# Tying a background task, scores, counts and running sums' products to their place in the list

## The chip, the core and the metric

The kernel runs on one core of a Trainium2 chip. A core has five engines with a queue of instructions each: TensorE (PE, products), VectorE (DVE, elementwise work), ScalarE (ACT, functions and copies), GpSimd (POOL, here mostly the issue of transfers) and SyncE (SP, transfers only). An engine takes its instructions strictly in the order in which the program lists them for it. The metric is the device time of one execution in microseconds (us), as a median over several executions.

## What is computed

A matrix of features `x` of 2708 x 512 goes through four layers on one weighted graph `adj` of 2708 x 2708, all in fp32. Every layer ends in a residual sum and a layernorm. Cut to what matters here:

```python
deg = maximum((adj != 0).sum(-1), 1.0)               # how many neighbours each row has
# layer 0: x = layernorm(x + (inc @ x) / inc.sum(-1)), with inc made from adj
# layer 1:
type_sum = adj @ x                                   # the gates' input and the second branch
h = x @ W_sa
s_left, s_right = h @ a_sa[0, :512], h @ a_sa[0, 512:]        # the scores
e = where(adj != 0, exp(-leaky_relu(s_left[:, None] + s_right[None, :], 0.01)), 0.0)
attn = e / (e.sum(axis=1, keepdims=True) + 1e-05)    # e.sum: the running sums
x_a, x_b = attn @ h, adj @ (x @ W_gcnb) + b_gcnb
x = layernorm(x + sigmoid(gate_a * x_a + gate_b * x_b))
# layer 2: x = layernorm(x + sum over hops k of adj^k @ x @ weight[k])
# layer 3: a_norm = rsqrt(deg) * (adj + I) * rsqrt(deg);  x = layernorm(x + relu((a_norm @ x + x) @ W + b))
```

## The kernel before

`adj` is taken as 2 x 2 blocks of half its size (1354). A product with it is made as seven products of half size over sums and differences of the blocks (s1 to s4), where eight would be direct. The result columns are cut into ranges: in the layer-1 sweeps 384, 384, 256 and 330 columns. One range takes seven *slots*, one for each product, in the order P1, P7, P5, P6, P4, P3, P2; a slot is 10 steps of k (128 rows of `adj`), each with two instructions per half (`step`, L462, "a row" is four of these), and what is over 1280 rows follows in `rest` (L480, L486). TensorE accumulates in banks `accu`, `accc`, `accd`, `acca`; ScalarE copies them out (L516), VectorE adds them into the tiles C11 to C22 and their sums (`add`, L523; names such as `P1c`, `C21`, `W`), and dense products (`dense`, `ps_d`, L610) multiply these by the weights.

The kernel is written as a list. `at(pos, fn, hold=False)` (L179) puts a function down at a position, counted in slots; at the end the list is sorted by position and the functions are called in that order (L1723). A scheduler then orders the instructions of each engine by its own estimates of when they are ready and how much depends on them, so the order in the program is not the order of the list. The exception is `hold`: every instruction that such a function issues gets an order-only dependence on the instruction that stands before it on the same engine in the list (L1730). It can't be put ahead of that one, while instructions of functions without `hold` may still move.

The stages are at positions `S = [0, 28, 35, 91, 119, 147, 175]` (L687): layer 0, the plain product of layer 1 for the last range (S[1]), the attention of layer 1 (S[2], four ranges of seven slots), and then the later layers. The change touches S[1] and S[2]:

- `score` (L902): VectorE multiplies a tile of x by the score vectors and sums along the row (L907); `score_rows` (L929) turns a column of scores into a row (`to_rows`, L921: TensorE transpose `ps_r` L924, ScalarE copy, POOL store); SyncE loads those rows again for the attention.
- `pair` in `extra1` (L970): signs (ScalarE L973), squares (L974) and counts (VectorE L980) of the last range, for `deg`.
- In S[2] each block of `adj` is masked: ScalarE makes `e` (L1143, L1144), VectorE multiplies (L1145), makes s1 to s4 (`comb`, L407) and adds up running sums over rows (`add_run`, L766 to L770). `run_sums` (L777) reduces those over partitions by products with a vector of ones (`rs`, L783), for h=1 and h=0 of each range.
- The *background task* (L1048 to L1129) runs in S[2] beside the attention: for the 512 columns of each of two groups, ten rounds of k and one of the rest. A round: `back_load` (four transfers of 256 KB issued on POOL, L1059, into the tiles bk_0 to bk_3, which have one buffer each), `back_tally` (signs L1072, squares L1073 on ScalarE, counts `dg` L1075 on VectorE), `back_sums` (four VectorE operations L1095 which overwrite the tiles, and four stores to DRAM on POOL, L1096, which later layers load as `z<-As`). The next round's loads need those tiles and so the stores' end. A group ends with `back_end` (TensorE products `ds`, L1103) and `back_rows`.

Of the kernel before, what the change touches and what calls it, by code (L numbers as in the profile page):

```python
# [25 lines left out]
P = 128  # L26
EPS = 1e-5
NH = 1354
KT = 11
# [32 lines left out]
def wt(k):  # L62
    return min(P, NH - k * P) if k < KT else P
# [8 lines left out]
def gnn_kernel(ctx: ExitStack, tc: tile.TileContext, x, adjT, w_sa, a_sa, w_gcn, b_gcn, wab, bab, w_hop, w_out,  # L72
# [106 lines left out]
    def at(pos, fn, hold=False):  # L179

        def go():
            n = len(nc.cur_bb.bb.instructions)
            fn()
            held.update(range(n, len(nc.cur_bb.bb.instructions)))

        events.append((pos, len(events), go if hold else fn))
# [590 lines left out]
    def run_sums(R0, n, h, after):  # L777

        ps = bank("rs", [P, 4])
        t = run.pop((R0, h))  # L780
        ts = list(range(R0 // P, (R0 + n + P - 1) // P))
        for i, k in enumerate(ts):
            nc.tensor.matmul(ps[: wt(k), i : i + 1], t[:, k * P - R0 : k * P - R0 + wt(k)], ones_f, start=True,  # L783
                             stop=True)
        r = small.tile([P, 4], F32, name="rd", bufs=4)
        for i, k in enumerate(ts):
            after(r[: wt(k), i : i + 1], ps[: wt(k), i : i + 1], h * KT + k, wt(k))
            rd[h * KT + k] = r[:, i : i + 1]
# [113 lines left out]
    def score(t, w, got, js):  # L902
        x1 = got.pop(t)
        junk = nat("vy")
        for j in js:
            for e in range(2):
                nc.vector.scalar_tensor_tensor(junk[:w, :HD], x1[:w, e * HD : (e + 1) * HD], 1.0, V[j, e][:w],  # L907
                                               ALU.mult, ALU.mult, accum_out=sc2[:w, t, e, j : j + 1])
# [20 lines left out]
    def score_rows(R0, h, ts):  # L929
        q = slice(h * KT + ts[0], h * KT + ts[-1] + 1)  # L930
        to_rows(s_left[:, q], len(ts), SROW[R0, h])
# [8 lines left out]
    got1 = {}  # L940
# [5 lines left out]
    for R0, n in RANGES:  # L946
        full = R0 == RANGES_A[0][0]
        for h in (1, 0):
            ts = tiles_of(R0, n)
            for k in ts:  # L950
                p = S[1] + 0.55 + 0.21 * i
                at(p, lambda t=h * KT + k: get_x1(t))
                at(p + 0.25, lambda t=h * KT + k, w=wt(k), js=range(4 if full else 2): score(t, w, got1, js))
                i += 1
            at(p + 0.26, lambda a=(h * KT + ts[0], len(ts), False): scores_end(*a))
            if full:
                at(p + 0.26, lambda a=(h * KT + ts[0], len(ts), True): scores_end(*a))
            at(p + 0.8, lambda R0=R0, h=h, ts=ts: score_rows(R0, h, ts))
    at(p + 0.27, scores_over)
    for i, (h, k) in enumerate((h, k) for g in (4, 0) for h in (0, 1) for k in range(g, g + 4)):  # L960
        p = S[2] + 1.6 + 1.3 * i
        at(p, lambda t=h * KT + k: get_x1(t))
        at(p + 0.4, lambda t=h * KT + k: score(t, P, got1, (2, 3)))
        if k % 4 == 3:
            at(p + 0.41, lambda a=(h * KT + k - 3, 4, True): scores_end(*a))

    def extra1(pb, r, R0, n, A):
        ts = tiles_of(R0, n)

        def pair(keys, w=P):  # L970
            m = pool.tile([P, 2, D], BF, name="sg", tag="nat", bufs=6)
            for h, key in enumerate(keys):
                nc.scalar.activation(m[:w, h, :n], A[(r,) + key][:w, :n], AF.Sign)  # L973
            nc.scalar.activation(m[:w, :, :n], m[:w, :, :n], AF.Square)  # L974
            if R0 not in deg:
                deg[R0] = d = pool.tile([P, 2, D], BF, name="dg", tag="nat", bufs=6)
                nc.vector.tensor_copy(d[:w, :, :n], m[:w, :, :n])
            else:
                d = deg[R0]
                nc.vector.tensor_tensor(d[:w, :, :n], d[:w, :, :n], m[:w, :, :n], ALU.add)  # L980

        for k in range(KW):
            at(pb + 0.1 + 0.8 * k / KT, lambda k=k: pair((("11", k), ("21", k))))
            at(pb + 3.9 + 0.8 * k / KT, lambda k=k: pair((("12", k), ("22", k))))
        for key, w in (("r", KA), ("r32", 32)):
            at(pb + 4.8, lambda key=key, w=w: pair(((key, 0), (key, 1)), w))

        def end(h):
            d = deg[R0]
            ps = bank("ds", [P, 4])  # L990
            for i, q in enumerate(ts):
                wq = wt(q)
                nc.tensor.matmul(ps[:wq, i : i + 1], d[:, h, q * P - R0 : q * P - R0 + wq], ones_bf[:, 0:1], start=True,
                                 stop=True)
            for i, q in enumerate(ts):
                wq = wt(q)
                o = rdeg[:wq, h * KT + q : h * KT + q + 1]
                nc.vector.tensor_scalar(o, ps[:wq, i : i + 1], 1.0, None, ALU.max)
                nc.vector.tensor_scalar(diag[:wq, h, q : q + 1], o, 1.0, None, ALU.add)
                nc.vector.reciprocal(o, o)  # L1000

        def rows(h):
            to_rows(rdeg[:, h * KT + ts[0] : h * KT + ts[-1] + 1], len(ts),
                    DROW[h][0, ts[0] * P : (ts[-1] + 1) * P].rearrange("(k i) -> k i", i=P))

        at(pb + 5.2, lambda: end(1))
        at(pb + 5.9, lambda: rows(1))
        at(pb + 5.2, lambda: end(0))
        at(pb + 5.9, lambda: rows(0))
# [81 lines left out]
    def back_sums(i0, k):  # L1091
        a11, a21, a22, a12 = back["t"]
        for m, o, a, b, op in (("s1", a22, a21, a22, ALU.add), ("s3", a21, a11, a21, ALU.subtract),
                               ("s2", a11, a22, a11, ALU.subtract), ("s4", a12, a12, a11, ALU.subtract)):
            nc.vector.tensor_tensor(o, a, b, op)  # L1095
            nc.gpsimd.dma_start(out=SD[m][k * P : (k + 1) * P, i0 : i0 + D], in_=o)  # L1096

    def back_end(i0):
        d = back.pop("d")
        ps = bank("ds", [P, 8])  # L1100
        for h in range(2):
            for i in range(4):
                nc.tensor.matmul(ps[:, 4 * h + i : 4 * h + i + 1], d[:, h, i * P : (i + 1) * P], ones_bf[:, 0:1], start=True,  # L1103
                                 stop=True)
        for h in range(2):
            q = slice(h * KT + i0 // P, h * KT + i0 // P + 4)
            o = rdeg[:, q]
            nc.vector.tensor_scalar(o, ps[:, 4 * h : 4 * h + 4], 1.0, None, ALU.max)
            nc.vector.tensor_scalar(diag[:, h, i0 // P : i0 // P + 4], o, 1.0, None, ALU.add)
            nc.vector.reciprocal(o, o)  # L1110

    def back_rows(i0, h):
        q = h * KT + i0 // P
        to_rows(rdeg[:, q : q + 4], 4, DROW[h][0, i0 : i0 + D].rearrange("(k i) -> k i", i=P))

    p = S[2] + 1.3
    for i0, _ in RANGES_B:
        at(p, back_start)
        for k in range(KW):
            at(p, lambda i0=i0, k=k: back_load(i0, k))  # L1120
            at(p + 0.6, back_tally)
            at(p + 0.7, lambda i0=i0, k=k: back_sums(i0, k))
            p += 1.13
        at(p, lambda i0=i0: back_rest_load(i0))
        at(p + 0.6, back_rest_tally)
        at(p + 0.85, lambda i0=i0: back_end(i0))
        at(p + 0.9, lambda i0=i0: back_rows(i0, 0))
        at(p + 0.95, lambda i0=i0: back_rows(i0, 1))
        p += 1.13  # L1129

    def start2b():
# [15 lines left out]
    def extra2(pb, r, R0, n, A):  # L1147
        def rows(h):
            row[R0, h] = tmp("row")
            m = (n + P - 1) // P  # L1150
            src = SROW[R0, h][0:1, :]
            nc.sync.dma_start(out=row[R0, h][:, : m * P].rearrange("p (k i) -> p k i", i=P),
                              in_=bass.AP(tensor=src.tensor, offset=src.offset, ap=[[0, P], [P, m], [1, P]]))

        def share(o, s, t, w):
            nc.vector.tensor_scalar(o, s, 1e-5, None, ALU.add)
            nc.vector.reciprocal(o, o)
            if R0 == RANGES_A[0][0]:
                nc.vector.tensor_tensor(o, o, gate[:w, t, 0:1], ALU.mult)

        at(pb - 1.6, lambda: rows(0))
        at(pb - 1.0, lambda: rows(1))
        at(pb + 5.2, lambda: run_sums(R0, n, 0, share))
        at(pb + 4.7, lambda: run_sums(R0, n, 1, share))

    def finish_x2(y, x1, w, t, h, r0):

# [562 lines left out]
    for n, i in enumerate(list(nc.cur_bb.bb.instructions)):  # L1730
        p = last if n < 3 * strict else done if n in held else {}
# [44 lines left out]
```

## Time and profile before

| | |
|---|---|
| median of 3 runs | 2932.55 us (2932.35 to 2941.14) |
| the profiled execution | 2930.68 us, span 2928.9 us, mean granted clock 0.988 |
| busy: TensorE, VectorE, ScalarE, POOL | 97%, 78%, 23%, 22% of the span |
| layer-1 sweeps S[1] and S[2] in the trace | about 434 to 552 us, and 552 to 1017 us |
| TensorE busy in 400 to 1000 us, by windows of 100 us | 91.4, 97.6, 95.7, 94.0, 90.5, 85.2 us |

A line of the profile names an engine, the operation, its output `<-` its inputs, and the line of the kernel. A wait reads: engine, tile and line that waited, `<-` the engine, tile and line that released it. "x8" means so many instructions. `bk`, `sg` and `dg` are the background task's tiles (`sg` and `dg` also name those of `pair`), `run` is a running sum, `a` a block of `adj`, and `As` is where the background task stores.

### The profile page before, as it was taken

The page shows a single profiled execution, that of the slowest core. Times are in us where ns is not written, and L with a number is a line of the kernel's source. Part 1 is how long each engine was busy: PE and PEld are TensorE (multiplying, and loading weights), DVE is VectorE, ACT ScalarE, POOL GpSimd, SP SyncE. Part 2 cuts the span into 40 slices and gives each one's busy share as a digit, 9 for nine tenths or more (in the row PEclk, how much of TensorE's full clock was granted, in tenths as well). Part 3 has the DMA queues.
Part 4 walks back from the last instruction along what each step waited for, and adds up shares of the span by engine and source line. Part 5 has one row for each costly group of instructions (what it writes and reads, how often), then busy time and mean ns, then how long its engine had stood idle before and what let it go on. Part 6 is the DMA issues. An engine that isn't in the chain of part 4 may idle for free.

```text
span 2928.9 us, 38864 instructions
## 1 busy us (share of the span) xinstructions
PE 2832.2 (97%) x11159; PEld 1913.9 (65%) x11159; DVE 2292.8 (78%) x5890; ACT 661.3 (23%) x1314; POOL 650.8 (22%) x1175
## 2 busy tenths in 40 slices
PE   7999999999989899999999999999999999999998
PEld 5655666556576678777666666666666666656665
DVE  6898688676667657677599877987878877899986
ACT  4554214765557311201200000000000100100001
POOL 0123233222232210213202224021230221501102
PEclk9999999999999999999999999999999999999999
DMA  7666466466566565577767768566675565854652
GB/s 225 194 204 186 140 206 205 138 206 190 168 203 197 164 183 146 176 221 244 228 177 240 211 196 257 166 184 213 192 251 165 177 202 176 251 152 138 182 140 79
DMA packets 404959, 554.41 MB, mean 189 GB/s; under 512 B 68752, under 2 KB 350556, under 8 KB 404744
## 3 DMA queue, kind: packets, MB, share of 16 engines
q1 hardware_dynamic: 330976, 391.33, 45.8%
q0 software_dynamic: 56032, 148.83, 15.4%
q10 hardware_dynamic: 17736, 11.76, 1.4%
q8 instruction: 89, 1.46, 0.2%
q14 instruction: 126, 1.03, 0.1%
HBM read 468.02 MB, written 83.65 MB: 188 GB/s over the span
## 4 chain that ended last, share of the span: by engine, by line
PE 71%; DVE 12%; issue 6%; DMA 6%; POOL 3%; ACT 1%; SPq 1%; POOLq 0%; DVEq 0%; ACTq 0%
PE accd L1356 13%; PE accu L1356 13%; PE accc L1356 12%; PE ps_d L610 6%; PE acca L1356 6%; PE accd L462 4%; PE accc L462 3%; PE accr L1427 3%; PE accu L462 3%; DMA bk<-in_adjT 2%; PE acca L462 2%; DVE z L1301 2%; DMA As<-bk 1%; PE accr L1431 1%; PE ps L649 1%
## 5 line engine op out<-in xcount | busy, mean ns | idle before, releaser
L1301 DVE TENSOR_TENSOR z<-z 128x339 f32<-128x339 f32 (+2 forms) x1176 | 538.4, 490 | 20.4 <-PE accu L1356 10.6
L1374 ACT COPY q<-accu 128x339 f32<-128x339 f32 (+2 forms) x105 | 41.6, 429 | 1056.7 <-PE accu L1356 836.2
L1356 PE MATMUL accc<-s,t 128*128 128x339 f32 (+2 forms) x784 | 233.5, 439 | 0.2 <-DVE s L1301 0.2
L1356 PE MATMUL accu<-z,t 128*128 128x339 f32 (+2 forms) x784 | 227.7, 436 | 4.2 <-DVE z L1301 3.0
L1356 PE MATMUL accd<-z,t 128*128 128x339 f32 (+2 forms) x784 | 227.8, 436 | 1.7 <-DVE q L1438 1.4
L1356 PE MATMUL accc<-z,t 128*128 128x339 f32 (+2 forms) x784 | 226.8, 436 | 0.5 <-ACT q L1374 0.5
L564 POOL TENSOR_TENSOR rstd<-rstd,neg_half 128x1 f32<-128x1 f32 (+3 forms) x91 | 59.7, 656 | 702.0 <-DVE rstd L563 446.9
L1356 PEld LDWEIGHTS accu<-z,t 128*128 128x128 f32 x784 | 148.1, 190 | 70.1 <-DVE z L1301 6.1
L1356 PEld LDWEIGHTS accc<-s,t 128*128 128x128 f32 x784 | 146.8, 190 | 70.7 <-issue 10.2
L1356 PEld LDWEIGHTS accd<-z,t 128*128 128x128 f32 x784 | 148.1, 190 | 66.7 <-DVE q L1438 2.3
L1356 PEld LDWEIGHTS accc<-z,t 128*128 128x128 f32 x784 | 148.2, 190 | 64.8 <-ACT q L1374 1.0
L1380 DVE TENSOR_TENSOR q<-q,accd 128x338 f32<-128x338 f32 (+2 forms) x140 | 67.9, 485 | 148.3 <-PE accd L1356 148.0
L1301 DVE TENSOR_TENSOR s<-z 128x339 f32<-128x339 f32 (+2 forms) x392 | 178.0, 490 | 7.5 <-PE accc L1356 3.2
L1575 POOL DMA_DIRECT2D Y<-y x192 | 104.7, 552 | 330.0 <-DVE y L1570 289.2
L407 DVE TENSOR_TENSOR a<-a,a 128x384 f32<-128x384 f32 (+2 forms) x240 | 118.0, 516 | 5.3 <-DMA a<-in_adjT 4.3
L1143 ACT ACTIVATE e<-row,s_right 128x384 f32<-128x384 f32 (+5 forms) x176 | 94.8, 566 | 41.0 <-DVE a L1145 11.6
L1145 DVE SCALAR_TENSOR_TENSOR a<-a,e 128x384 f32<-128x384 f32 (+2 forms) x160 | 76.9, 508 | 34.1 <-ACT e L1144 34.0
L569 ACT ACTIVATE ld<-ld,rstd 128x512 f32<-128x512 f32 (+3 forms) x45 | 36.5, 813 | 263.9 <-DVE rstd L566 98.1
L1438 DVE TENSOR_TENSOR q<-q,accr 128x338 f32<-128x338 f32 (+2 forms) x160 | 69.1, 485 | 22.8 <-PE accr L1431 22.7
L1380 DVE TENSOR_TENSOR q<-q,accu 128x338 f32<-128x338 f32 (+2 forms) x175 | 79.2, 485 | 3.9 <-ACT q L1374 2.6
L774 DVE SCALAR_TENSOR_TENSOR s<-a,row 128x384 f32<-128x384 f32 (+2 forms) x152 | 75.3, 508 | 6.0 <-ACT row L759 6.0
L1144 ACT ACTIVATE e<-e 128x384 f32<-128x384 f32 (+5 forms) x176 | 78.9, 475 | 1.4
(699 smaller groups left out, 5907.5 us busy)
## 6 DMA issues: line engine op xcount, KB each, us to landing
z<-As SPq DMA_DIRECT2D x320, 169.5 KB
z<-As SPq DMA_DIRECT2D x320, 169.0 KB
z<-in_adjT SPq DMA_DIRECT2D x240, 169.5 KB
z<-in_adjT SPq DMA_DIRECT2D x240, 169.0 KB
a<-in_adjT SPq DMA_DIRECT2D x160, 192.0 KB
bk<-in_adjT POOLq DMA_DIRECT2D x80, 256.0 KB, 4.6
As<-bk POOLq DMA_DIRECT2D x80, 256.0 KB, 3.2
z<-As SPq DMA_DIRECT2D x160, 128.0 KB
```

The source lines that it names most:

```text
L407: nc.vector.tensor_tensor(A[r, dst, k][:, :n], A[r, a, k][:, :n], A[r, b, k][:, :n], op)
L462: nc.tensor.matmul(B[home, c][:, :n], X[STAT[p], k][:, c * P : (c + 1) * P], A[r, MOV[p], k][:, :n], start=bool(start and k == k0), stop=k ...
L610: nc.tensor.matmul(o, lhs(c), r, start=c == 0 and n == 0, stop=c == DC - 1, skip_group_check=True)
L774: nc.vector.scalar_tensor_tensor(t[:w, :n], a[:w, :n], 0.0, row[R0, h][:w, :n], ALU.is_gt, ALU.mult)
L1143: nc.scalar.activation(e[:w, :n], row[R0, h][:w, :n], AF.Prelu, bias=s_right[:w, t : t + 1], alpha=0.01)
L1144: nc.scalar.activation(e[:w, :n], e[:w, :n], AF.Exp, scale=-1.0)
L1145: nc.vector.scalar_tensor_tensor(a[:w, :n], a[:w, :n], 0.0, e[:w, :n], ALU.not_equal, ALU.mult)
L1301: nc.vector.tensor_tensor(d[:, :n], Z[x + (k,)][:, :n], Z[y + (k,)][:, :n], op)
L1356: nc.tensor.matmul(B[home][:, :n], stat(v, k), a[:, :n], start=bool(start and k == 0), stop=k == nk - 1, skip_group_check=True)
L1380: nc.vector.tensor_tensor(d[:, :n], s_[:, :n], B[home][:, :n], ALU.add)
L1427: nc.tensor.matmul(ps[r][:, :n], XA[:KA, c * P : (c + 1) * P], R[h, s][:KA, :n], start=True, stop=False, skip_group_check=True)
L1575: nc.gpsimd.dma_start(out=rows[:, :, f * P : (f + 1) * P], in_=o[32 * f : 32 * (f + 1), : m * P].rearrange("p (b d) -> p b d", d=P))
```

## The change

Functions of the list get `hold=True`, and some positions move. What they issue is the same as before.

```diff
-            at(p + 0.8, lambda R0=R0, h=h, ts=ts: score_rows(R0, h, ts))
+            at(p + 0.8, lambda R0=R0, h=h, ts=ts: score_rows(R0, h, ts), True)
...
-        at(p + 0.4, lambda t=h * KT + k: score(t, P, got1, (2, 3)))
+        at(p + 0.4, lambda t=h * KT + k: score(t, P, got1, (2, 3)), True)
...
-            at(pb + 0.1 + 0.8 * k / KT, lambda k=k: pair((("11", k), ("21", k))))
-            at(pb + 3.9 + 0.8 * k / KT, lambda k=k: pair((("12", k), ("22", k))))
+            at(pb + 0.1 + 0.8 * k / KT, lambda k=k: pair((("11", k), ("21", k))), True)
+            at(pb + 3.9 + 0.8 * k / KT, lambda k=k: pair((("12", k), ("22", k))), True)
         for key, w in (("r", KA), ("r32", 32)):
-            at(pb + 4.8, lambda key=key, w=w: pair(((key, 0), (key, 1)), w))
+            at(pb + 4.8, lambda key=key, w=w: pair(((key, 0), (key, 1)), w), True)
...
             at(p, lambda i0=i0, k=k: back_load(i0, k))
-            at(p + 0.6, back_tally)
-            at(p + 0.7, lambda i0=i0, k=k: back_sums(i0, k))
+            at(p + 0.65, back_tally, True)
+            at(p + 0.75, lambda i0=i0, k=k: back_sums(i0, k), True)
             p += 1.13
         at(p, lambda i0=i0: back_rest_load(i0))
-        at(p + 0.6, back_rest_tally)
-        at(p + 0.85, lambda i0=i0: back_end(i0))
-        at(p + 0.9, lambda i0=i0: back_rows(i0, 0))
-        at(p + 0.95, lambda i0=i0: back_rows(i0, 1))
+        at(p + 0.65, back_rest_tally, True)
+        at(p + 0.9, lambda i0=i0: back_end(i0), True)
+        at(p + 1.1, lambda i0=i0: back_rows(i0, 0), True)
+        at(p + 1.12, lambda i0=i0: back_rows(i0, 1), True)
...
-        at(pb + 5.2, lambda: run_sums(R0, n, 0, share))
-        at(pb + 4.7, lambda: run_sums(R0, n, 1, share))
+        at(pb + 6.5, lambda: run_sums(R0, n, 0, share), True)
+        at(pb + 5.05, lambda: run_sums(R0, n, 1, share), True)
```

`pb` is the first slot of a range and `p` runs on by 1.13 slots from round to round, from S[2] + 1.3 on. `rest` of h=1 is at pb + 5.0 and of h=0 at pb + 5.999, both unchanged. In the new program's order on TensorE, the `rs` of h=1 stands behind `rest` and one row of P3, where it stood ahead of the second half of P4; the `rs` of h=0 stands inside P2.

## The prediction

> **What bounds the kernel now.** I read the page first (TensorE is busy for 97% of the span), then the windows, then TensorE's waits and its timeline in the stage that the change edits, then the chain that leads to the longest of those waits. The windows (start:end and length in us, busy us of each engine with instructions, granted clock, DMA share, GB/s):
>
> ```profile
> core 0: us, PE busy (x) PEld busy (x) DVE busy (x) ACT busy (x) POOL busy (x), PEclk, DMA share, GB/s
> 800.00:900.00 100.00, 90.51 (x412) 74.89 (x411) 66.76 (x195) 62.18 (x130) 30.94 (x58) 0.95 0.65 203
> 900.00:1000.00 100.00, 85.16 (x329) 60.44 (x328) 69.98 (x178) 51.14 (x98) 28.02 (x53) 0.91 0.63 189
> 1000.00:1100.00 100.00, 100.00 (x421) 73.99 (x420) 55.62 (x145) 17.95 (x34) 16.18 (x26) 1.00 0.55 159
> ```
>
> From 1000 us on TensorE is full at clock 1.00, so a microsecond won or lost before that reaches the end one to one. The other windows from 400 us on read 91.4, 97.6, 95.7 and 94.0 busy: 45.6 us of TensorE idle in 400 to 1000, which is all that there is to win. TensorE's waits in 380 to 1020 us (what waits, for what: us in total, times, longest):
>
> ```profile
> PE rs L783 <- DVE run L770: 21.1, 4, 8.7
> PE ds L1103 <- DVE dg L1075: 6.7, 1, 6.7
> PE ps_d L610 <- ACT sg L1073: 6.0, 1, 6.0
> PE ps_r L924 <- DVE s_left L918: 4.8, 2, 4.5
> PE ps_n L593 <- DVE P1c L523: 3.7, 1, 3.7
> ```
>
> The first row is the running sums' product, four times, once in each range of the attention layer. Its timeline (start, us, line, in brackets the idle time before it):
>
> ```profile
> 630.50 1.04 PE L783 MATMUL rs<-ones_f,run 128*128 128x1 f32 x6 [4.28 <-DVE run L770]
> 631.40 4.29 PE L462 MATMUL accc<-a,T4D 128*128 128x384 f32 x8
> 758.05 1.41 PE L783 MATMUL rs<-ones_f,run 128*128 128x1 f32 x6 [5.97 <-DVE run L770]
> 870.66 0.98 PE L783 MATMUL rs<-ones_f,run 128*128 128x1 f32 x4 [8.72 <-DVE run L770]
> 914.18 1.19 PE L610 MATMUL ps_d<-T1B,P1c 128*128 128x256 f32 x2 [5.97 <-ACT sg L1073]
> 984.90 0.37 PE L1103 MATMUL ds<-ones_bf,dg 128*128 128x1 bf16 x8 [6.73 <-DVE dg L1075]
> ```
>
> The second line is what a wait costs afterwards: the same eight products took 2.74 us just before it. What made the sum late is in the chain of waits:
>
> ```profile
> 614.44 3.84 DMA As<-bk
> ...
> 618.57 5.90 DMA bk<-in_adjT
> ...
> 624.49 0.63 ACT sg L1072
> ...
> 628.58 1.87 DVE run L770 x4
> ...
> 630.50 1.04 PE rs L783 x6
> ```
>
> VectorE stood on a background tally (one store, then one load into the same buffer, then signs, square, add), and the last four running-sum adds were behind it. So the background round is a closed loop with one set of buffers, and TensorE meets it through VectorE's order.
>
> **What the Trainium skill says.** "Trainium Architecture — The Big Picture", section "Inside one NeuronCore": each engine has its own instruction stream and they meet only in semaphores. Hence what stands behind a waiting instruction waits too; the chain agrees (run behind dg). "TensorE: Matmul & The Clock Gate", Part 1: the clock is halved after an idle window of about 3.4 us, and wants about as long to come back. The trace agrees: 4.29 against 2.74 us behind a wait of 4.28. "DMA: Bandwidth & Descriptors", section on the SWDGE path: 2.0 us plus bytes over 436 GB/s, which makes an estimated 2.6 us for a 256 KB tile; the page of this kernel has medians of 3.2 (store) and 4.6 (load) and the chain 3.84 and 5.90, so I take the trace's.
>
> **The round, by rows.** From the issue of a round's last store (613.24) to the next tally's add (626.48) the chain has 13.2 us: store 3.84, load 5.90, sign 0.63, square 1.07 (L1073, at 625.38), the rest issue. With one add (L1075, 0.69 mean) and four sums (L1095, 0.69 each) behind it that is 13.2 + 3.4 = 16.7 us for a round in strict order. The timeline of VectorE has the last sums of rounds 11 to 20 and the last add from 821.7 to 984.8: 16.3 us each. TensorE goes through a round's 1.13 slots in 14.6 us at 384 columns (40 rows of four products at 1.29 us are 4 slots, 12.9 us each), 13.6 at 256 and 16.3 at 330. So in the last ranges the loop is the slower of the two.
>
> **The change, part by part.** No instruction is added or taken away: the counts of the two programs are equal on every engine, and the orders are equal up to about 415 us of the trace and, but for numbering, from about 1015 us on.
>
> *Layer-1 sweep (434 to 552 us): scores, score rows, pairs.* VectorE is at 80% in 400 to 500. The C-copies and adds come earlier there, so most of the 3.66 us wait of L593 at 440.24 goes, but the score rows (L924, waits 4.8 + 2.1) stand one to three rows (1 to 4 us) later behind the same VectorE work. I take -1.5 (from -5, both waits gone, to +1). The rows' stores on POOL and their loads on SP move with them; the attention layer reads them tens of us later, so they cost nothing; without that cover a row's store and load would stand in the path with some 8 us.
>
> *Range 0 (384 columns).* The product of h=1 now stands behind T4D, the rest and one row of B22A: about 7 us of TensorE later (T4D 2.74; the rest at L480 and L486 2.9 and 1.1, by the timeline at 635.53 to 639.1; a part of a row). Its sum, at 630.5 before, is met at 633: the wait of 4.28 and the cold clock (4.29 - 2.74 = 1.55) go, 5.8 us. What is late next: the add for C21 (L523) now stands on VectorE behind round 2's sums, and the dense product ps_d (L610) waits for it. Queued behind that add on VectorE are the add for W and the mask products of the next slot (L1145), which TensorE has in stock for a row or two. TensorE would be there at 641.7 - 5.8 = 635.9, the add is there at about 638, and a wait of over 2 us costs about 1 of clock: -2.7.
>
> *Range 1.* The wait of 5.97 and about 2 of clock go, so ps_d would come at 770.6 - 8 = 762.6. But C21 is now behind round 9's first tally. Round 6 ended at 723.8; three rounds at 16.7, less what overlaps, put that tally at about 770.5 to 772.4 (round 9 ended at 770.1 before). So a wait of about 9 us stands there, and the range loses 2.2 with its cold clock.
>
> *Ranges 2 and 3 (256 and 330 columns).* The waits of 8.72 and 0.78 turn into waits for C21 and W, behind round 14's sums (5.5 to 6.5); the wait at 914.18 stays (P1c stands behind round 16's sums, 6 to 7). They don't add up, since the account is settled at ds, where TensorE waited 6.73 before. Rounds of 16.7 in place of 16.3 and the 1.8 of round 9 put the last tally's add at 984.8 + 1.8 + 11 x 0.45 = about 992, 7 us later. Ahead of ds TensorE now has about 8 us more to do (T4D, rest, two rows), which it no longer has to do behind it. Together -0.8 against before, with a bound of -10 to +10, since a round that is 1 us shorter or longer counts ten times.
>
> *Background stores and row stores* on POOL are tied too: the four stores of a round now go out together before the next loads, which moves no landing by more than an issue of 0.54 us. SP's queue is not tied.
>
> *Sum.* Up to ps_d of range 1: -1.5 - 2.7 + 2.2 = -2.0. At ds: -0.8. Work that no longer follows a cold ds (rs, h=1) and what the first ranges give the loop earlier: 1 to 2. I take -3. The profiled execution (2930.68, span 2928.9) would go to 2927.7; the median shown is 1.9 above it, so **2929.5 us**. A difference under 0.3% (8.8 us) is about what a measurement of this kernel can't tell from none.
>
> **Rivals.** *A, the waits are gone for good.* VectorE's main work now stands ahead of each tally, so TensorE never meets the loop. For it: the rs waits are caused by order alone. Against: ds must follow the last tally, and the loop's own 16.3 us is no order's doing. It gives -21.1, and -6.0 of clock (four waits at 1.5), ds and the rest left as they are: about 2905. It needs rounds of under 15.5 us. *B, slower: each round gets longer.* The fixed order makes a round's store, load, both tallies and sums strictly follow each other, behind main operations that themselves wait for TensorE; at 16.7 + 1.5 = 18.2 a round, ten rounds end 19 us later than before, less 3 to 8 us of work moved ahead of ds: +12 to +16, about 2946. It decides from some 17.3 us a round. For it: VectorE in order behind adds that wait for TensorE, and TensorE behind them. Against: the main operations ahead are ready early in most rounds. *C, nothing changes:* unlikely, since the orders differ by whole rows in this stage.
>
> **How the numbers follow.** My case 0.44, A 0.27, B 0.28, C 0.01. My case has a spread of about 7 us around -3, which puts two tenths beyond -8.8 and little beyond +8.8: faster 0.27 + 0.09, slower 0.24 + 0.02, the rest of 0.38 within 0.3%. The range takes B to 2954 and half of A, from 2905 on. The likeliest case alone: 2920 to 2939.
>
> **What would show it.** Right: the waits of rs for run L770 fall from 21.1 to under 4; waits of ps_d L610 for C21 or W (DVE L523) of 15 to 25 us appear; ds waits 8 to 14; the sum of TensorE's idle in 400 to 1000 us stays within 40 to 48; last sums of rounds 11 to 20 are 16.5 to 17.3 apart. Wrong by A: rounds under 15.5 and windows 800 to 1000 over 95% busy. Wrong by B: rounds over 17.5, ds after 998, and DVE bk L1095 waiting for work that stands ahead of it and waits for TensorE. The prediction would also fail if the layer-1 sweep lost time, which I price at little.

## The result, and the profile after

The changed kernel takes 2939.78 us (median of 20 runs, 2932.93 to 2945.09), the kernel before beside it 2932.21 (20 runs, 2924.17 to 2941.14). The ratio is 1.0027, 95% interval 1.0019 to 1.0035: slower by 0.27%, some 7.6 us. That is inside the 0.3% that I had set as too small to tell, but with 20 runs each it can be told, and its sign is not the one of my 2929.5. The profiled execution took 2940.72 us with a span of 2938.9.

The windows of the changed kernel, with the columns as shown before:

```profile
400.00:500.00 100.00, 85.80 (x334) 57.48 (x333) 75.82 (x274) 21.67 (x51) 41.52 (x76) 0.93 0.72 220
...
900.00:1000.00 100.00, 81.50 (x315) 57.61 (x314) 76.10 (x182) 64.41 (x127) 30.99 (x58) 0.92 0.72 219
1000.00:1100.00 100.00, 100.00 (x431) 74.84 (x432) 52.50 (x153) 18.79 (x35) 19.57 (x33) 0.98 0.54 154
```

TensorE's idle time in 400 to 1000 us is 59.9 us, 45.6 before. Stage S[2] alone, from its first to its last product (which ends at 1029.5 us in the trace before, not at about 1017 as stated above), takes 486.1 us, 477.1 before; of the 9.0 us more, 8.5 are idle time of TensorE (43.1 against 34.6). From 1000 us on TensorE is full in both; the clock of 0.98 in that window comes right after the last wait, which ends at 1000.0. The waits of TensorE in 380 to 1040 us:

```profile
PE ps_d L610 <- DVE C L523: 24.3, 3, 11.4
PE ds L1103 <- DVE dg L1075: 13.5, 1, 13.5
PE ps_r L924 <- DVE s_left L918: 7.6, 2, 6.2
...
PE ps_d L610 <- DVE P1c L523: 5.0, 1, 5.0
```

The row of the running sums' product, 21.1 us before, has gone. In its place ps_d waits for C21 (the tile C of L523) in three ranges, and ds waits twice as long. The longest of the three and the last one in TensorE's timeline:

```profile
774.70 1.22 PE L610 MATMUL ps_d<-T1B,C 128*128 128x256 f32 x2 [11.44 <-DVE C L523]
...
999.97 0.38 PE L1103 MATMUL ds<-ones_bf,dg 128*128 128x1 bf16 x8 [13.46 <-DVE dg L1075]
```

And the chain of waits that ends in the first of them:

```profile
763.71 2.73 DMA As<-bk
...
767.01 4.13 DMA bk<-in_adjT
...
771.22 1.16 ACT sg L1072 x2
...
772.40 1.06 ACT sg L1073
...
773.49 0.69 DVE dg L1075
774.18 0.48 DVE C L523
...
774.70 2.50 PE ps_d L610 x5
```

It is the same loop as in the chain before: store, load, sign, square, count. Then VectorE waited at the count with the last running-sum adds behind it; now it waits with the add for C21 behind it. VectorE had been idle for 4.89 us when dg came.

The last sums of rounds 11 to 20 of the background end at 827.9 to 983.7 us, 17.3 us apart (before 821.7 to 969.8, 16.5 apart), and the products ds start at 1000.0 (before 984.9). Rounds are counted from 1 here; the prediction's rounds 2, 6, 9, 14 and 16 are counted from 0.

### The profile page after: what moved, and what is told of

Read it like the earlier page. It is cut to its first block, busy times and chain, and to the rows that moved or that the text cites. A ratio compares the mean times of both kernels' runs of the same rounds, so it can differ in the third digit from the quotient of the medians.

```text
span 2938.9 us, 38871 instructions
## 1 busy us (share of the span) xinstructions
PE 2829.1 (96%) x11159; PEld 1916.4 (65%) x11159; DVE 2294.5 (78%) x5890; ACT 662.4 (23%) x1314; POOL 649.7 (22%) x1175
## 4 chain that ended last, share of the span: by engine, by line
PE 68%; DVE 12%; DMA 9%; issue 6%; POOL 3%; ACT 2%; SPq 1%; ACTq 0%; POOLq 0%; DVEq 0%
PE accd L1356 12%; PE accu L1356 12%; PE accc L1356 12%; PE ps_d L610 6%; PE acca L1356 6%; PE accd L462 4%; PE accc L462 3%; PE accr L1427 3%; PE accu L462 3%; DMA bk<-in_adjT 2%; PE acca L462 2%; DMA As<-bk 2%; DVE z L1301 1%; DMA X<-o 1%; DVE vy L907 1%
## 5 line engine op out<-in xcount | busy, mean ns | idle before, releaser
L1301 DVE TENSOR_TENSOR z<-z 128x339 f32<-128x339 f32 (+2 forms) x1176 | 537.1, 488 | 21.1 <-PE accu L1356 10.7
L564 POOL TENSOR_TENSOR rstd<-rstd,neg_half 128x1 f32<-128x1 f32 (+3 forms) x91 | 59.9, 658 | 691.8 <-DVE rstd L563 438.1
```

Source lines behind the costliest of these rows:

```text
L1301: nc.vector.tensor_tensor(d[:, :n], Z[x + (k,)][:, :n], Z[y + (k,)][:, :n], op)
```

## The experiments

Each was run beside the kernel before on the same chip, and its ratio is to that (its median there was 2928.5 to 2932.2 us); the versions have 4 to 22 runs each. "Round" is the mean distance between the last sums of rounds 11 to 20 in the trace, "ds" the start of the second group's products there. Single traces differ: at about 380 us, up to where both programs have the same order, the changed kernel's trace is 3.6 us ahead of the one before. So a few us in a trace are not a finding, and the ratios carry the verdicts.

| run | median us | ratio (95%) | round us | ds us |
|---|---|---|---|---|
| kernel before (profiled) | 2932.21 | 1 | 16.5 | 985 |
| the change | 2939.78 | 1.0027 (1.0019 to 1.0035) | 17.3 | 1000 |
| background part alone | 2938.15 | 1.0023 (1.0015 to 1.0032) | 17.5 | 996 |
| products later and tied, alone | 2931.94 | 1.0002 (0.9994 to 1.0010) | 16.2 | 984 |
| score rows, pairs, scores tied, alone | 2930.59 | 1.0005 (0.9995 to 1.0014) | 16.4 | 985 |
| positions alone, no ties | 2926.80 | 0.9984 (0.9976 to 0.9993) | 16.3 | 984 |
| background's positions alone | 2924.57 | 0.9981 (0.9973 to 0.9988) | 16.1 | 979 |
| background tied at its old positions | 2935.68 | 1.0016 (1.0009 to 1.0022) | 17.0 | 998 |
| change, POOL free | 2938.52 | 1.0024 (1.0017 to 1.0032) | 17.6 | 1001 |
| change, ScalarE free | 2942.61 | 1.0043 (1.0030 to 1.0056) | 17.5 | 998 |
| change, VectorE free | 2938.01 | 1.0025 (1.0016 to 1.0034) | 17.2 | 1001 |
| change, ScalarE and VectorE free | 2931.45 | 1.0002 (0.9994 to 1.0010) | 16.6 | 987 |

### Which part costs

My theory after the result: the ties on the background lengthen its rounds, and the rounds bound the stage. The rivals: the layer-1 sweep lost the time (its window 400 to 500 shows 5.6 us more idle time), or the products moved later did.

*The background's part alone* (the diff's lines from `back_tally` to `back_rows`):

> The kernel before with only the background's part of the change (tally, sums, rest, end and rows tied, at their new positions). Theory 1, the tied background makes each round longer (17.2 us against 16.3 between rounds 11 and the last add): the whole loss is here, +6 to +14 us on the kernel before, rounds of 17 us or more, and waits of rs for run L770 stay above 15 us. Theory 2, the layer-1 sweep lost the time: within 3 us of before. Theory 3, the products moved later cost it (TensorE meets the C21 add): within 3 us of before.

+0.23%, about 6.8 of the 7.6 us, with rounds of 17.5: the first theory. A detail of it failed: the rs waits fell to 11.8 us in two places, since in the other ranges C21 was already what came late (ps_d for C: 19.6 us).

*The products alone* (the last two lines of the diff):

> The kernel before with only the running sums' products listed later and tied; the background stays free. Theory 1: the rs waits (21.1 us) go to under 4, rounds stay at about 16.3 us, and what is gained is what the free scheduler doesn't give back at ps_d and ds: -4 to -15 us. If the loop bounds the stage whatever the order (my prediction's account at ds): within 4 us of before, with ds or ps_d waiting 15 us or more. Theory 3: +3 to +8.

No difference, and the waits show why:

```profile
PE ps_d L610 <- DVE C L523: 18.0, 4, 9.5
PE ds L1103 <- DVE dg L1075: 9.4, 1, 9.4
```

The 21.1 us of rs are gone (0.4 left), and 18.0 at ps_d and 2.7 more at ds stand in their place, with the rounds as before. This is the account that I had made for the whole change: it holds for this part of it.

*Score rows, pairs and second scores alone* (the first hunks of the diff):

> The kernel before with only score rows, pairs and second scores tied. Theory 2: TensorE's idle time in 400 to 500 us rises from 8.6 to about 14 us and the whole kernel by 4 to 8 us. Theory 1: the idle time rises, but the whole kernel by 0 to 4 us.

TensorE's idle time in 400 to 500 us rises to 12.1 us (8.6 to 10.9 in the ten traces in which this sweep is as before), and no change of the kernel's time can be told. A further run below looks for a loss that the loop hides.

*All positions, no ties:*

```diff
-            at(p + 0.65, back_tally, True)
+            at(p + 0.65, back_tally)
...
-        at(pb + 5.05, lambda: run_sums(R0, n, 1, share), True)
+        at(pb + 5.05, lambda: run_sums(R0, n, 1, share))
```

> All new positions of the background and the running sums' products, nothing tied. Theory 1 (it is the ties that lengthen the round): within 4 us of before or faster, rounds of about 16.3 us. Rival (the positions do it): +5 to +10 us, as the whole change.

Faster by 0.16%. So the positions gain and the ties lose more, 0.43% from this version to the whole change. *The background's positions alone* and *its ties at the old positions* complete the square:

> The kernel before with the background's new positions alone, nothing tied, running sums' products as before. If the gain of all positions (-4.6 us) is the background's: -3 to -6 us. If it needs the products moved as well: within 2.5 us of before. If it comes from leaving the products free, within 2.5 us too.

> The kernel before with the background tied at its old positions. If the ties cost (+6.8 us at the new positions): +5 to +12 us, rounds of 17 us or more. If it is the new positions together with the ties: within 3 us of before.

The positions alone give -0.19%, the ties alone +0.16%, both together +0.23%. The two don't simply add: at the new positions the ties cost 0.42%, at the old ones 0.16%. In the first the rs waits stay at 23.0 us; what went is the wait of ps_d for sg (6.0 before) and half of that of ds (3.1).

### Is the loop the bound?

```diff
     def back_load(i0, k):
+        if k > 0:
+            return
         back["t"] = ts = back_tiles()
```

> The kernel before with the background's loads left out after the first round of each group (the later rounds count and sum what stands in the tiles; stores stay), so that a round no longer waits for a load. If the loop bounds the attention stage: ds and ps_d no longer wait for the background, TensorE's idle time in 600 to 1000 us falls from 34.6 to under 20 us, the kernel by 12 to 28 us. If order alone caused the waits: under 5 us faster.

2879.19 us, ratio 0.9819 (0.9803 to 0.9836): 51 us, far more than I expected. Its windows:

```profile
600.00:700.00 100.00, 100.00 (x360) 64.86 (x359) 70.84 (x175) 58.20 (x107) 14.57 (x27) 1.00 0.48 151
...
800.00:900.00 100.00, 98.53 (x451) 82.24 (x450) 85.78 (x236) 75.73 (x154) 21.60 (x40) 1.00 0.59 190
900.00:1000.00 100.00, 99.55 (x423) 71.58 (x422) 66.91 (x176) 39.83 (x78) 22.22 (x40) 1.00 0.54 155
```

All four windows (700 to 800 reads 100.00 too) are full or nearly so at clock 1.00, though every main function is at the place in the list that it had. So the waits of TensorE in all of the attention stage, under whatever name, come from the background's loads: from the loop that they close, or from the traffic that they make, which this run takes away too.

*The changed kernel without those loads:*

> The changed kernel with the same loads left out. If the ties cost only because they lengthen a loop that bounds: as fast as or faster than the kernel before without loads, within 4 us. If the tied order costs by itself (engines in order behind work that waits for TensorE): 5 to 10 us slower than that one.

2884.75 us, ratio 0.9836 (0.9820 to 0.9851), 5.6 us above the other one (the four runs of each don't overlap). By my expectation this speaks for a cost of the tied order by itself; its wait for C falls to 1.2 us and that of ds to 2.5. *Score rows and pairs tied, without the loads:*

> The kernel before with score rows, pairs and second scores tied, and the background's loads left out after the first round of each group. If the loss of the layer-1 sweep was real and hidden only because TensorE then waits less for the background's loop: 3 to 6 us slower than the kernel before without those loads (2879.2), where with the loads the same ties cost nothing that could be measured. If that loss is made up inside the sweep itself: within 2 us of 2879.2.

2878.91 us, ratio 0.9825 (0.9810 to 0.9840), level with the 2879.19. So the ties of the layer-1 sweep are no part of the loss that these runs can tell; where their idle time is made up is not shown. The 5.6 us stand with the rest of the ties, and no run separates them further.

### What in the ties lengthens a round?

The ties on one engine at a time were left out where the dependence is added:

```diff
-        p = last if n < 3 * strict else done if n in held else {}
+        p = last if n < 3 * strict else done if n in held and i.engine != mybir.EngineType.Pool else {}
```

> The changed kernel with the ties left out on POOL alone (the background's stores and the row stores may move). If the four stores, held in line behind stores of xa that wait for ScalarE (4.6 us at 822.2 to 826.8), lengthen the round: rounds under 17 us, 2 to 6 us faster than the changed kernel. If the ties on ScalarE and VectorE do it: within 2 us of the changed kernel (2939.8).

> The changed kernel with the ties left out on ScalarE alone (signs, squares and row copies may move). In the changed kernel the time from a round's last sum to the next round's first sign is 9.1 us against 7.8 before, and the rest of a round is no longer than before. If the sign's place in ScalarE's line, behind main work that waits for TensorE, is the cause: back to 8.3 or less, rounds of 16.6 or less from round 11 on, 4 to 9 us faster than the changed kernel. If not: within 2 us of it.

> The changed kernel with the ties left out on VectorE alone (counts, sums, scores may move). If the counts' and sums' place in VectorE's line lengthens the round: sign to last sum below 7.7 us (8.2), rounds of 16.6 or less, 4 to 9 us faster than the changed kernel. If ScalarE's line does it: within 3 us of the changed kernel.

None of the three gives anything back, against what I expected of one of them (ScalarE's median is even some 3 us higher, but its interval overlaps that of the change). With ScalarE free, the time from a round's last sum to the next first sign falls from 9.1 to 7.4 us (7.8 before), but from there to the last sum it rises from 8.2 to 10.1. With VectorE free it is 9.5 and 7.7. What one engine gains the other gives back. So both at once:

> The changed kernel with the ties left out on ScalarE and VectorE together; those on TensorE and POOL stay. If the background waits in the lines of both engines and either alone is enough to hold it up: rounds of 16.6 or less from round 11 on, ds at 990 us or earlier, within 4 us of the positions alone (2926.8), 8 to 15 us faster than the changed kernel. If the ties on TensorE cost it: within 4 us of 2939.8, with rounds of 16.6 or less.

Back to the kernel before (1.0002), with ties left on TensorE and POOL. Either engine's ties are enough to hold the rounds up. It is not back within 4 us of the positions alone, as I had expected: the intervals (0.9984 there) don't overlap, so some 5 us stay with the ties that are left, and those on POOL alone had been worth nothing. How they do it is to be seen in the same round in both traces. ScalarE before (round 15 of the sums):

```profile
875.87 1.80 ACT L1072 ACTIVATE sg<-bk 128x512 bf16<-128x512 f32 x3 [7.97 <-DMA bk<-in_adjT]
877.58 1.04 ACT L1073 ACTIVATE sg<-sg 128x1024 bf16<-128x1024 bf16 x1
878.52 0.61 ACT L1072 ACTIVATE sg<-bk 128x512 bf16<-128x512 f32 x1
```

and after:

```profile
895.93 1.15 ACT L1072 ACTIVATE sg<-bk 128x512 bf16<-128x512 f32 x2 [10.95 <-DMA bk<-in_adjT]
...
897.36 1.04 ACT L1073 ACTIVATE sg<-sg 128x1024 bf16<-128x1024 bf16 x1
898.30 1.13 ACT L1072 ACTIVATE sg<-bk 128x512 bf16<-128x512 f32 x2
```

The first sum of the round on VectorE, before and after:

```profile
877.91 0.68 DVE L1095 TENSOR_TENSOR bk<-bk,bk 128x512 f32<-128x512 f32 x1
...
899.47 0.69 DVE L1095 TENSOR_TENSOR bk<-bk,bk 128x512 f32<-128x512 f32 x1 [0.35 <-ACT sg L1072]
```

Before, the scheduler had put three signs together (bk_1, bk_0, bk_2), so the first started at the second landing (875.8 us) and the sum that overwrites the third of these tiles could run at once. Tied, the signs stand as they were written: bk_0, bk_1, square, bk_3, bk_2. But the loads of a round are issued as the tiles' stores end, bk_2, bk_1, bk_0, bk_3, and land at 891.8, 894.9, 895.9 and 897.6. So the first sign waits for the third tile (it starts within 0.1 us of the third landing in 14 of the 20 rounds; in the others it waits for its place on ScalarE), and the first sum (bk_2 overwritten) for the last sign of all. On VectorE a count stands ahead of the first sum in all 20 rounds (at 898.43 us in this one; before, a sum came first in 9 of the 20), and VectorE's waits of counts for squares grow from 27.6 to 55.4 us in 560 to 1000 us. Both counts stand ahead of all four sums in 6 rounds only; a tie allows that, for it holds an instruction behind one other, which may itself be free to move.

*The same without a tie's help: sums first.* The signs in one function, the sums directly behind, squares and counts last:

```diff
-            at(p + 0.6, back_tally)
-            at(p + 0.7, lambda i0=i0, k=k: back_sums(i0, k))
+            at(p + 0.6, back_signs)
+            at(p + 0.61, lambda i0=i0, k=k: back_sums(i0, k))
+            at(p + 0.7, back_tally)
```

It was put into the kernel before, into the positions alone, into the background's positions alone, and into the whole change:

> The kernel before with the four sums directly behind the signs and squares and counts after them; no position of the change, nothing tied. If the shorter loop is the gain of the version with positions and this step (2911.5): 10 to 20 us faster than before. If the later products are needed for it: 3 to 10 us faster, with 15 us or more of rs waits left.

> The positions of the change without ties, and in a round the four sums directly behind the signs, with squares and counts after them (stores and so the next loads no longer wait for anything but signs and sums). If the loop bounds: rounds 1 to 3 us shorter (13.5 to 15.5 from round 11 on), ds 5 to 25 us earlier, the kernel 5 to 15 us faster than the one with the positions alone, 2912 to 2922. If it doesn't: within 3 us of that one (2926.8).

> Sums directly behind the signs, and the background's new positions, nothing tied, the running sums' products where they were before. If the products' place is worth something once the loop is shorter: slower than the version with all positions (2911.5), about 2914.8 or more. If the gain of the background's positions (-5.7 us) adds to that of the sums (-17.2 us): about 2908.

> The whole change, ties included, with the four sums directly behind the signs and squares and counts after them. If the loop's length is what TensorE waits for: sign to last sum shorter by 1.5 to 3 us, the kernel 10 to 22 us faster than the changed one (2918 to 2930), still 5 to 15 us slower than the same step with positions alone (2911.5), since the ties keep the first sign late. If the ties' other effects dominate: within 5 us of 2939.8.

| sums first, in | median us | ratio (95%) | round us |
|---|---|---|---|
| the kernel before | 2914.84 | 0.9941 (0.9929 to 0.9954) | 15.9 |
| all positions | 2911.54 | 0.9932 (0.9917 to 0.9947) | 16.1 |
| the background's positions | 2906.14 | 0.9926 (0.9910 to 0.9942) | 15.4 |
| the whole change, tied | 2934.13 | 1.0013 (1.0005 to 1.0021) | 16.8 |

Sums first alone give 0.59%; the intervals of the first three overlap, so that the positions add to it, or the later products don't, is not shown. Rounds 11 to 20 got shorter by less than I expected (the 15.5 us at most were reached only in the third), and most of the gain came earlier: in the first version's trace the last sum of round 20 is 16.8 us earlier than before, and 12.0 of these had been won by round 11. Whether it is the shorter loop or what stands behind the counts on VectorE that gains there is not separated. In the tied version little came (0.14% on the change, and the intervals overlap): in half of the rounds the first sign still stands at the third landing (845.7 and 879.2 us in its trace, with the third tile landed at 845.6 and 879.2), and in all of them the first sum is behind the last sign.

*All ties kept, a round written in the order of landing.* This differs from the last row in the order of signs and sums; squares and counts also move, by 0.1 slot, to directly behind them:

```diff
+        sign(a22); sign(a21); sums("s1", a22, a21, a22, ALU.add)      # bk_2, bk_1
+        sign(a11); sums("s3", a21, a11, a21, ALU.subtract)            # bk_0
+        sums("s2", a11, a22, a11, ALU.subtract)
+        sign(a12); sums("s4", a12, a12, a11, ALU.subtract)            # bk_3
+        squares and counts
```

(shortened: `sign` stands for the activation call, and each sum issues its store)

> The whole change with all its ties, and each round listed in the order in which its tiles land (bk_2, bk_1, bk_0, bk_3), each sum right behind the last sign that it needs, squares and counts last. It differs from the tied version with sums first (2934.1) only in the order of signs and sums. If the ties cost because they fix an order in which the first sign waits for the third tile to land (from round 12 on in the changed kernel's trace): first sign 1.5 to 3 us earlier after the last sum, the sums' stores earlier, rounds of 13.5 to 15.8, the kernel at 2905 to 2920. If being tied behind the main work is what costs: within 4 us of 2934.1.

2906.15 us, ratio 0.9910 (0.9893 to 0.9927): 28 us faster than the tied version with the other order, and 0.9% faster than the kernel before. ScalarE and VectorE of this kernel in one round:

```profile
836.47 0.63 ACT L1089 ACTIVATE sg<-bk 128x512 bf16<-128x512 f32 x1 [1.24 <-DMA bk<-in_adjT]
837.98 0.63 ACT L1090 ACTIVATE sg<-bk 128x512 bf16<-128x512 f32 x1 [0.87 <-DMA bk<-in_adjT]
839.96 0.63 ACT L1092 ACTIVATE sg<-bk 128x512 bf16<-128x512 f32 x1 [1.35 <-DMA bk<-in_adjT]
843.66 0.63 ACT L1095 ACTIVATE sg<-bk 128x512 bf16<-128x512 f32 x1 [3.08 <-DMA bk<-in_adjT]
```

```profile
839.64 0.70 DVE L1086 TENSOR_TENSOR bk<-bk,bk 128x512 f32<-128x512 f32 x1
...
844.33 0.69 DVE L1086 TENSOR_TENSOR bk<-bk,bk 128x512 f32<-128x512 f32 x1 [1.79 <-ACT sg L1095]
```

In this round each sign follows its landing, three sums are done before the fourth tile is there, and its sum comes 0.7 us behind its sign. Both counts stand behind all four sums in every round, where in the tied version with sums first a count stood among the sums in 12 of 20; so the 28 us belong to the order of the whole round, and the signs' share of them was not run alone. Rounds are 15.2 us, and from first sign to last sum 5.7 (8.2 in the changed kernel). One part of my expectation missed: the first sign is not nearer to the last sum (9.5 us), because in some rounds (at 826.4, with all tiles landed by 819.9) the background is now ahead of its place in the list and waits there. What is left of TensorE's waits for it is 5.2 us at ds and 4.7 at ps_d for C.

So being tied need not cost: with the order of landing the fully tied kernel is level with the fastest untied version (2906.15 and 2906.14 us). What cost was mostly the order that the ties fix. An untied kernel listed in the order of landing was not run, so whether ties cost something in that order stays open; without the loads it was 5.6 us.

## Why the prediction was wrong

**What held.** The waits moved as foretold, by name and nearly by size: rs under 4 us (none left), ps_d for C21 15 to 25 (24.3), ds 8 to 14 (13.5). So did the premise that TensorE meets the loop whatever its own order; rival A, the waits gone for good, is excluded by the products alone (1.0002). The account at ds is sound in its form: from ds to the stage's last product it was 44.0 us before and is 37.9 after (28 products moved ahead), and 15.1 us later less 6.1 makes the 9.0 by which the stage ends later in the trace.

**The step that failed** is "Rounds of 16.7 in place of 16.3 and the 1.8 of round 9 put the last tally's add at 984.8 + 1.8 + 11 x 0.45 = about 992". It came at 999.9. Both terms were mis-sized. On the prediction's measure, from the last sum of round 11 to that add, the rounds are 17.2 (16.3 before), and the background entered them 6.2 us late (round 11's last sum at 827.9 against 821.7), not 1.8: 984.8 + 6.2 + 10 x 0.9 makes the 999.9. The 6.2 are what ranges 0 and 1 had lost: round 11's tiles had landed by 803.1, and its first sign, at 821.3, is as much later than before as TensorE's products are there. The 0.9 are in the step from a round's last sum to the next first sign (9.1 us against 7.8; the rest of the round is 0.5 shorter). I had taken the chain of one untied round and put the sums behind it, as if the first tile to land were the first to be signed. The order of the signs stands in `back_tally`, and I didn't lay it beside the order of the loads. So "the loop's own 16.3 us is no order's doing" is wrong too: with the signs in the order of landing and the sums ahead of the counts a round takes 15.2.

**Sums and readings.** The term 11 x 0.45 fits neither the ten rounds between the two instants nor 16.7 less 16.3; ten times 0.4 would have put the add at 990.6, further off. TensorE's 14.6 us for a round at 384 columns counts the products of the slots alone; without the loads the first two ranges take 121.0 and 120.1 us for seven slots, 19.5 and 19.4 a round, so there TensorE is slower than the loop. The 13.6 and 16.3 of the narrower ranges are near what that run shows (13.8 and 17.0), so only at 256 columns is the loop clearly the slower. And the 45.6 us of idle time were not "all that there is to win": the kernel before without the loads won 51.

**The ranges**, by the first product of each in both traces: range 0 was to win 2.7 us and lost 1.6 (wait for C21 5.0, not some 2); range 1 was to lose 2.2 and lost 4.5 (11.4, not 9); the account at ds, with ranges 2 and 3, was to be -0.8 and is +9.0. The mechanism, C21 behind a tally or its sums, was the right one in ranges 0 to 2, and these came later than I had them. A clock cost of 1 us behind a wait of 2 is not what the trace shows: behind the wait of 2.13 us at 976.25 four products took 1.36 us, 1.27 elsewhere. **The layer-1 sweep**, -1.5 in my sum: none measured (1.0005, and -0.3 us without the loads). **The stores on POOL**, priced at nothing: nothing (1.0024 against 1.0027). **The idle time** was to stay in 40 to 48 us and is 59.9.

**Rival B** had the right sign, the right mark (ds after 998) and the threshold of 17.3 us a round which the rounds just reach (its mark of 17.5 they don't). Its cause was work ahead that waits for TensorE, and its third mark didn't come: VectorE's waits of bk L1095 fell from 30.2 to 3.8 us in 560 to 1000 us. A share of that cause may stand in the 5.6 us without the loads and in the 6 of 20 rounds whose first sign waits for its place on ScalarE, but the order within the round is worth more: 28 us between two fully tied versions.

## What to carry to other kernels

When an edit fixes an order, hold the fixed order of consumers against the order in which their inputs really arrive, tile by tile; here signs written in another order than the loads made the first sign wait for the third tile in 14 of 20 rounds, and the first sum for the last sign in all. When a wait moves to another name with nearly the same sum, look for the closed loop behind both names and shorten that (here the steps from the loads to the first store). Free two engines together before concluding that neither's order matters.

## What the runs showed of the hardware that was not expected

Waiting cost TensorE more than the wait. In stage S[2], from its first to its last product, the kernel before takes 477.1 us and the one without the loads 432.3, for the same 1668 products. Of the 44.8 us between them 32.7 are idle time (34.6 against 1.9), and 12.2 are products that took longer, at a mean granted clock of 0.96 against 1.00. I take these 12 us for the clock after many short waits; that the stage also moves less data without the loads (159 against 184 GB/s) was not separated. The rest of the 51 us lies outside the stage, where single traces differ by as much.
